# Attention in a two-layer Macaron kernel: the next head's products moved between a head's third scores and its first transposes

## The chip, the cores and the metric

The kernel runs on one core of a Trainium2 chip, in one launch. The metric is the device time of that launch in microseconds (us), the median of several runs. The engines are PE (matrix multiply; PEld is its loading of weights), DVE (vector), ACT (scalar, exponentials and copies), POOL (a second vector engine without access to PE's output banks) and SP (issues transfers). PE writes into PSUM, eight banks of 512 float32 columns each, and DVE and ACT read the results from there.

## The reference

Activations `x` are 1024 tokens of 512 channels, all in float32. Six residual blocks follow each other: a mixture-of-experts FFN, attention, the same FFN again, a LoRA FFN, a Mamba-type scan block, the LoRA FFN again. The change concerns attention alone:

```python
q = einsum('bsd,de->bse', hidden, wq).reshape(B, S, 32, 192)
k, v = ...                       # 32 heads of 128 each, from hidden @ wkv
scores = einsum('bqhd,bkhd->bhqk', q[..., :128], k) * 192 ** -0.5
scores = where(causal, scores, -1e30)
probs = softmax(scores, axis=-1)
attn = einsum('bhqk,bkhd->bqhd', probs, v).reshape(B, S, 32 * 128)
out = einsum('bse,ed->bsd', attn, wo)
```

## The kernel before

The 32 heads go in eight groups of four. The transposed, normalized activations `hT` stay in SBUF. For each group `load_heads` brings four weight tiles (`w_v`, `w_q`, `w_k`, `w_o`) into a pool of four buffers, and POOL forms sums and differences of them (`sums`, L621, and a scaling of `w_q`, L655). `products` (L244 on) computes a 2x2 block product with seven block multiplications in place of eight: each is written to a bank of the small PSUM pool, and DVE (ACT for the first) adds it into the result at L263 to L280.

Per group the values of four heads are computed once (`mm_v`, L795). Per head `products` computes `qT` and `kT` together (`mm_qk`, L819): seven block products of two 128x512 matmuls each. Then come eight query tiles of 128 tokens. For query tile `qt`:

- `scores` (L696) multiplies `qT` with the first `(qt + 1) * 128` keys (L701), in a two-bank tile of the pool `pbig` (two such tiles); DVE adds the causal mask (L708) and takes the negated row maximum (L712); ACT takes the exponential and its row sum (L715); DVE inverts the sum (L716) and scales the probabilities `pr` (L717).
- `attend` (L734) transposes `pr` block by block on PE (L156, up to four blocks in one bank), and copies them to `pT` (L744 on DVE, L746 on ACT). After the fourth and the eighth query tile `values` (L720) multiplies `v` with `pT` (L725) and copies the result to `oT` (L732).

`attend` of a tile runs behind `scores` of the next: the list `pending` holds the tiles not yet attended, and `flush(1)` leaves one of them. After the last tile of a group's fourth head `project_out` (L756) multiplies the four `oT` with `w_o`.

PSUM is split in two pools: `pbig`, two tiles of two banks, for scores alone, and `psml`, four single banks, for all else (products, transposes, outputs, projections). A tile of a pool can only be written when the reader of the tile that had its place is done.

The order on each engine is not the order of the text. A scheduler takes all instructions with their dependences and the order of the text as their priority, assigns the places of the pools, and writes one fixed sequence per engine, in which an instruction may stand ahead of earlier ones that were not ready in its plan. On the chip each engine goes through its sequence in order and waits on semaphores.

## Time and profile before

| | us |
|---|---|
| median of three runs (3053.02 to 3056.49) | 3054.58 |
| the profiled execution | 3056.72 |
| its span, first to last instruction | 3054.9 |
| attention, from the first head's products to the last projection | about 205 to 1721 |
| PE busy in the span | 2861.3 |
| DVE busy in the span | 1719.6 |
| ACT busy in the span | 717.1 |

The profile is one execution, taken on the chip. A row of the groups gives the line, engine and operation, the tiles written and read, the number of instructions, their busy time and mean duration, and the idle time of the engine just before them with what ended it. A row of a timeline gives the start in us from the start of the span, the time until the last instruction of the row ends, and in brackets the idle time before it. A float32 matmul appears as two records. A row of the stages gives the stretch and its length, then busy time and number of instructions of PE, PEld, DVE, ACT and POOL, the granted PE clock as a share of full speed, the share of transfers and their rate.

### The profile page before, as it was taken

The page shows a single profiled execution, that of the slowest core. Times are in us where ns is not written, and L with a number is a line of the kernel's source. Part 1 is how long each engine was busy: PE and PEld are TensorE (multiplying, and loading weights), DVE is VectorE, ACT ScalarE, POOL GpSimd, SP SyncE. Part 2 cuts the span into 40 slices and gives each one's busy share as a digit, 9 for nine tenths or more (in the row PEclk, how much of TensorE's full clock was granted, in tenths as well). Part 3 has the DMA queues.
Part 4 walks back from the last instruction along what each step waited for, and adds up shares of the span by engine and source line. Part 5 has one row for each costly group of instructions (what it writes and reads, how often), then busy time and mean ns, then how long its engine had stood idle before and what let it go on. Part 6 is the DMA issues. An engine that isn't in the chain of part 4 may idle for free.

```text
span 3054.9 us, 29302 instructions
## 1 busy us (share of the span) xinstructions
PE 2861.3 (94%) x10691; PEld 1524.3 (50%) x10691; DVE 1719.6 (56%) x3183; ACT 717.1 (23%) x1381; POOL 790.1 (26%) x601
## 2 busy tenths in 40 slices
PE   5979999999999999999999796899999999999988
PEld 3434645556455554555644343455555555555544
DVE  3156546365463645636445414676776767767673
ACT  1212123031220312203122121422222222222220
POOL 3230101001010010100100123054555545555451
PEclk8989999999999999999999897999999999999999
DMA  8420100001000010000100542222332322323210
GB/s 279 124 72 1 42 14 28 28 1 42 14 28 28 1 42 14 28 28 1 42 14 28 197 131 66 76 90 90 96 97 89 105 90 97 98 88 105 95 42 28
DMA packets 102175, 196.95 MB, mean 64 GB/s; under 512 B 9040, under 2 KB 34800, under 8 KB 102032
## 3 DMA queue, kind: packets, MB, share of 16 engines
q1 hardware_dynamic: 84896, 157.15, 15.8%
q0 software_dynamic: 6240, 20.45, 2.6%
q10 hardware_dynamic: 10896, 17.47, 1.5%
q8 instruction: 87, 1.43, 0.2%
q14 instruction: 56, 0.46, 0.1%
HBM read 176.17 MB, written 18.87 MB: 64 GB/s over the span
## 4 chain that ended last, share of the span: by engine, by line
PE 80%; DVE 10%; POOL 4%; issue 3%; DMA 2%; ACT 1%; POOLq 0%; DVEq 0%; SPq 0%; ACTq 0%
PE ps_in L227 14%; PE ps_m L819 13%; PE ps_o L725 9%; PE ps_wo L760 7%; PE ps_s L701 6%; PE ps_tr L156 6%; PE ps_out L1230 6%; PE ps_m L795 6%; PE ps_e L506 5%; PE ps_y L1186 3%; PE ps_up L238 2%; DVE nm L712 1%; PE ps_st L1204 1%; DVE xc L1039 1%; DVE e_seg L1143 1%
## 5 line engine op out<-in xcount | busy, mean ns | idle before, releaser
L701 PE MATMUL ps_s<-kT,qT 128*128 128x512 f32 (+3 forms) x768 | 305.9, 503 | 33.0 <-ACT pr L715 30.2
L715 ACT ACTIVATE pr<-ps_s,nm 128x128 f32<-128x128 f32 (+7 forms) x256 | 189.7, 741 | 503.7 <-DVE nm L712 444.5
L725 PE MATMUL ps_o<-pT,v 128*128 128x512 f32 (+3 forms) x768 | 266.5, 497 | 1.3 <-ACT pT L746 0.5
L1230 PE MATMUL ps_out<-w_out,yg 128*128 128x512 f32 x512 | 241.6, 616 | 0.0
L227 PE MATMUL ps_in<-hT,w_g 128*128 128x512 f32 x512 | 227.1, 596 | 8.6 <-issue 8.6
L227 PE MATMUL ps_in<-hT,w_x 128*128 128x512 f32 x512 | 225.8, 593 | 0.0
L1168 POOL TENSOR_TENSOR cs<-cT,dd 128x1024 f32<-128x1024 f32 x56 | 181.8, 3247 | 164.9 <-PE ps_y L1186 140.4
L760 PE MATMUL ps_wo<-w_o,oT 128*128 128x512 f32 x512 | 222.1, 592 | 0.0
L725 PEld LDWEIGHTS ps_o<-pT,v 128*128 128x128 f32 x768 | 141.3, 191 | 135.0 <-issue 92.8
L746 ACT COPY pT<-ps_tr 128x256 f32<-128x256 f32 (+2 forms) x192 | 91.9, 479 | 477.8 <-PE ps_tr L156 472.4
L655 POOL TENSOR_SCALAR w_q<-w_q 128x1024 f32<-128x1024 f32 x16 | 44.3, 2770 | 605.8 <-DMA w_q<-in_wq_dram 605.2
L712 DVE TENSOR_REDUCE nm<-ps_s 128x1 f32<-128x128 f32 (+7 forms) x256 | 193.2, 755 | 5.5
L701 PEld LDWEIGHTS ps_s<-kT,qT 128*128 128x128 f32 x768 | 123.3, 190 | 124.7 <-ACT pr L715 65.6
L156 PEld LDWEIGHTS ps_tr<-ident,pr 128*128 128x128 f32 x1152 | 134.3, 141 | 97.5 <-issue 54.1
L156 PE MATMUL ps_tr<-ident,pr 128*128 128x128 f32 x1152 | 164.6, 274 | 19.5 <-DVE pr L717 18.5
L506 PE MATMUL ps_e<-w_all,xt_s 128*128 (+1 forms) x368 | 169.3, 604 | 0.0
L227 PEld LDWEIGHTS ps_in<-hT,w_g 128*128 128x128 f32 x512 | 96.6, 190 | 128.1 <-issue 128.1
L1143 DVE TENSOR_TENSOR_SCAN e_seg<-dd,eye 128x1024 f32<-128x1024 f32 x64 | 154.3, 2411 | 8.6 <-PE ps_y L1186 7.1
L717 DVE TENSOR_SCALAR pr<-pr,sm 128x128 f32<-128x128 f32 (+7 forms) x256 | 155.1, 606 | 4.6
L227 PEld LDWEIGHTS ps_in<-hT,w_x 128*128 128x128 f32 x512 | 97.0, 190 | 120.9 <-issue 120.4
L760 PEld LDWEIGHTS ps_wo<-w_o,oT 128*128 128x128 f32 x512 | 96.2, 190 | 115.7 <-issue 115.7
L1039 DVE SCALAR_TENSOR_TENSOR xc<-ps_in,conv,xc 128x511 f32<-128x511 f32 (+2 forms) x192 | 141.5, 737 | 17.9 <-ACT xc L1035 17.6
(252 smaller groups left out, 4378.1 us busy)
## 6 DMA issues: line engine op xcount, KB each, us to landing
dd<-decay SPq DMA_DIRECT2D x128, 512.0 KB, 4.6
w_all<-in_w_e_dram SPq DMA_DIRECT2D x16, 1024.0 KB, 9.7
outs<-y_e ACTq DMA_DIRECT2D x46, 256.0 KB, 3.5
w_v<-in_wkv_dram SPq DMA_DIRECT2D x8, 1024.0 KB, 5.3
w_q<-in_wq_dram SPq DMA_DIRECT2D x32, 256.0 KB, 4.3
w_k<-in_wkv_dram SPq DMA_DIRECT2D x8, 1024.0 KB, 5.2
w_o<-in_wo_dram SPq DMA_DIRECT2D x8, 1024.0 KB, 5.2
w_x<-in_in_wt_dram SPq DMA_DIRECT2D x8, 1024.0 KB, 7.7
```

The lines of the kernel that those rows point to most:

```text
L156: nc.tensor.transpose(ps[:, i * P : (i + 1) * P], src(i), ident)
L227: nc.tensor.matmul(ps[:, cols : cols + n], lhsT=w[:, k, c0 : c0 + P], rhs=hT[:, k, t0 : t0 + n], start=(k == 0), stop=(k == KT - 1),)
L506: nc.tensor.matmul(ps, lhsT=xt[:, k, :], rhs=w_all[:, bass.ds(ep, 1), k, :].rearrange("p e c -> p (e c)"), start=(k == 0), stop=(k == KT - 1),
L701: nc.tensor.matmul(ps[:, j : j + m], lhsT=qT[:, qt * P : (qt + 1) * P], rhs=kT[:, j : j + m], start=True, stop=True,)
L712: nc.vector.tensor_reduce(nm, ps[:, :n], AX.X, ALU.max, negate=True)
L715: nc.scalar.activation(pr[:, :n], ps[:, :n], AF.Exp, bias=nm, accum_out=sm)
L725: nc.tensor.matmul(ps[:, lo:512], lhsT=v[:, kb, hh * P : (hh + 1) * P], rhs=pT[:, kb, lo:512], start=(kb == 0), stop=(kb == last),)
L760: nc.tensor.matmul(ps, lhsT=heads[hh][:, t * P : (t + 1) * P], rhs=w[:, hh, :], start=(hh == 0), stop=(hh == HG - 1),)
L795: nc.tensor.matmul(ps[:, t * 256 : (t + 1) * 256], lhsT=right[i][:, k, (j + t) * P : (j + t + 1) * P], rhs=left[i][:, k, :], start=(first ...
L819: nc.tensor.matmul(ps, lhsT=left[i][:, k, hh * P : (hh + 1) * P], rhs=right[i][:, k, :], start=(first and k == 0), stop=(last and k == 1), ...
L1143: nc.vector.tensor_tensor_scan(e.rearrange("p h l -> p (h l)"), dd[:, 0, :], eye8.rearrange("p h l -> p (h l)"), 0.0, ALU.mult, ALU.add,)
L1230: nc.tensor.matmul(po, lhsT=yg[:, k, :], rhs=w_o[:, k, :], start=(k == 0), stop=(k == 3))
```

## The change

The loop over groups and heads is turned into one loop over 32 heads, with the work taken apart into `begin_group` (loads, sums, values), `begin_head` (products) and `query_tile`. Three things change in the order and the places:

- The next head's `begin_head` (with the next group's `begin_group` before it where a group ends) is called between the scores of a head's third tile and the first flush behind it.
- Two tiles stay pending in place of one (`flush(2)`).
- Scores of up to 512 columns (the first four tiles) take a single bank of `psml`; only the last four take a two-bank tile of `pbig`.

```diff
             def scores(qT, kT, qt):
                 n = (qt + 1) * P
-                ps = pbig.tile([P, S], F32, tag="pb", name="ps_s")
+                if n > 512:
+                    ps = pbig.tile([P, S], F32, tag="pb", name="ps_s")
+                else:
+                    ps = psml.tile([P, 512], F32, tag="ps", name="ps_s")
...
-            for g in range(AH // HG):
+            def begin_group(g):
+
                 if g == 0:
-                    ld = first
...
+                    return dict(first, v=v_first, heads=[])
+                ld = load_heads(g)
+                v = vp.tile([P, NT, 512], F32, tag="v", name="v")
...
+            def begin_head(gr, g, hh):
+
+                hd = {"gr": gr, "g": g, "hh": hh}
+                hd["qT"] = qT = qkp.tile([P, S], F32, tag="qT", name="qT")
+                hd["kT"] = kT = qkp.tile([P, S], F32, tag="kT", name="kT")
...
+                products(mm_qk, qT[:, :512], qT[:, 512:], kT[:, :512], kT[:, 512:])
...
+            def query_tile(hd, qt, between=None):
+                gr, g, hh = hd["gr"], hd["g"], hd["hh"]
+                if qt % 4 == 0:
+                    hd["pT"] = ptp.tile([P, qt + 4, 512], F32, tag=f"pT{qt}", name="pT")
+                pr = scores(hd["qT"], hd["kT"], qt)
...
+                state["pending"].append((pr, qt, gr["v"], hh, hd["pT"], hd["oT"], done))
+                if between is not None:
+                    between()
+                flush(2)
...
+            def begin(n):
+                g, hh = n // HG, n % HG
+                if hh == 0:
+                    nxt["group"] = begin_group(g)
+                nxt["head"] = begin_head(nxt["group"], g, hh)
+
+            begin(0)
+            for n in range(1, AH + 1):
+                hd = nxt["head"]
+                for qt in range(NT):
+                    query_tile(hd, qt, (lambda: begin(n)) if qt == 2 and n < AH else None)
             flush(0)
```

The engines' sequences for POOL and SP are the same in both programs, line numbers aside. Behind attention those of PE, DVE and ACT are the same too.

More of the change, by code (lines that the diff above doesn't have):

```diff
@@ L671, in attention @@
             state = {"pending": []}
-            v = vp.tile([P, NT, 512], F32, tag="v", name="v")
+            v_first = vp.tile([P, NT, 512], F32, tag="v", name="v")
             def first_v(t):
@@ L676, in first_v @@
                 tokens_times(ps, t, first["wv"], 512)
-                nc.scalar.copy(v[:, t, :], ps)
+                nc.scalar.copy(v_first[:, t, :], ps)
             def pair():
@@ L771, in project_out, with mm_v @@
                     after.flush()
-            for g in range(AH // HG):
+            def begin_group(g):
                 if g == 0:
-                    ld = first
-                else:
-                    ld = load_heads(g)
-                    v = vp.tile([P, NT, 512], F32, tag="v", name="v")
-                    wv = ld["wv"]
-                    left_v = sums(
-                        cp,
-                        wv[:, :2, :256],
-                        wv[:, 2:, :256],
-                        wv[:, :2, 256:],
-                        wv[:, 2:, 256:],
-                        "sv",
-                    )
-                    ld["left"] = left_of_heads(ld, left)
-                wog = ld["wo"]
-                for j in (0, 2) if g else ():
-                    def mm_v(ps, i, first, last, j=j, left=left_v):
+                    return dict(first, v=v_first, heads=[])
+                ld = load_heads(g)
+                v = vp.tile([P, NT, 512], F32, tag="v", name="v")
+                wv = ld["wv"]
+                left_v = sums(
+                    cp,
+                    wv[:, :2, :256],
+                    wv[:, 2:, :256],
+                    wv[:, :2, 256:],
+                    wv[:, 2:, 256:],
+                    "sv",
+                )
+                ld.update(left=left_of_heads(ld, left), v=v, heads=[])
+                for j in (0, 2):
+                    def mm_v(ps, i, first, last, j=j):
                         for t in range(2):
@@ L797, in mm_v @@
                                     lhsT=right[i][:, k, (j + t) * P : (j + t + 1) * P],
-                                    rhs=left[i][:, k, :],
+                                    rhs=left_v[i][:, k, :],
                                     start=(first and t == 0 and k == 0),
@@ L810, in attention @@
                     )
-                left_qk = ld["left"]
-                heads = []
-                for hh in range(HG):
-                    qT = qkp.tile([P, S], F32, tag="qT", name="qT")
-                    kT = qkp.tile([P, S], F32, tag="kT", name="kT")
-                    def mm_qk(ps, i, first, last, hh=hh, left=left_qk):
-                        for k in range(2):
-                            nc.tensor.matmul(
-                                ps,
-                                lhsT=left[i][:, k, hh * P : (hh + 1) * P],
-                                rhs=right[i][:, k, :],
-                                start=(first and k == 0),
-                                stop=(last and k == 1),
-                                skip_group_check=not first,
-                            )
-                    products(mm_qk, qT[:, :512], qT[:, 512:], kT[:, :512], kT[:, 512:])
-                    oT = op.tile([P, S], F32, tag="oT", name="oT")
-                    heads.append(oT)
-                    pT = None
-                    for qt in range(NT):
-                        if qt % 4 == 0:
-                            pT = ptp.tile(
-                                [P, qt + 4, 512], F32, tag=f"pT{qt}", name="pT"
-                            )
-                        pr = scores(qT, kT, qt)
-                        done = None
-                        if hh == HG - 1 and qt == NT - 1:
-                            done = lambda w=wog, hs=heads, last=(g == AH // HG - 1): project_out(w, hs, last)
-                        state["pending"].append((pr, qt, v, hh, pT, oT, done))
-                        flush(1)
@@ new lines, in begin_group, with mm_qk @@
+                return ld
+            def begin_head(gr, g, hh):
+                hd = {"gr": gr, "g": g, "hh": hh}
+                hd["qT"] = qT = qkp.tile([P, S], F32, tag="qT", name="qT")
+                hd["kT"] = kT = qkp.tile([P, S], F32, tag="kT", name="kT")
+                def mm_qk(ps, i, first, last):
+                    for k in range(2):
+                        nc.tensor.matmul(
+                            ps,
+                            lhsT=gr["left"][i][:, k, hh * P : (hh + 1) * P],
+                            rhs=right[i][:, k, :],
+                            start=(first and k == 0),
+                            stop=(last and k == 1),
+                            skip_group_check=not first,
+                        )
+                products(mm_qk, qT[:, :512], qT[:, 512:], kT[:, :512], kT[:, 512:])
+                hd["oT"] = oT = op.tile([P, S], F32, tag="oT", name="oT")
+                gr["heads"].append(oT)
+                return hd
@@ new lines, in query_tile @@
+            def query_tile(hd, qt, between=None):
[3 more added lines that the diff above has]
+                pr = scores(hd["qT"], hd["kT"], qt)
+                done = None
+                if hh == HG - 1 and qt == NT - 1:
+                    done = lambda: project_out(gr["wo"], gr["heads"], g == AH // HG - 1)
+                state["pending"].append((pr, qt, gr["v"], hh, hd["pT"], hd["oT"], done))
+                if between is not None:
+                    between()
+                flush(2)
@@ L843, in attention @@
+            nxt = {}
+            def begin(n):
[8 more added lines that the diff above has]
+                    query_tile(hd, qt, (lambda: begin(n)) if qt == 2 and n < AH else None)
             flush(0)
```

## Prediction

> **What bounds the kernel now.** I read the page first: its engine totals, then the costliest groups with the idle time before each.

> ```profile
> PE 2861.3 (94%) x10691; PEld 1524.3 (50%) x10691; DVE 1719.6 (56%) x3183; ACT 717.1 (23%) x1381; POOL 790.1 (26%) x601
> ...
> L701 PE MATMUL ps_s<-kT,qT 128*128 128x512 f32 (+3 forms) x768 | 305.9, 503 | 33.0 <-ACT pr L715 30.2
> ...
> L156 PE MATMUL ps_tr<-ident,pr 128*128 128x128 f32 x1152 | 164.6, 274 | 19.5 <-DVE pr L717 18.5
> ```

> The kernel is bound by PE. All that attention still gives away is PE's idle time ahead of the scores (33.0 us, they wait for an exponential to free a score buffer) and ahead of the transposes (19.5 us, they wait for the scaled probabilities). The change touches attention alone, so I asked for the stages: 205 us is the first head's products, 1721 us the end of the last output projection.

> ```profile
> 205.00:1721.00 1516.00, 1461.92 (x4942) 803.97 (x4941) 799.28 (x1651) 330.65 (x762) 147.09 (x80) 1.00 0.09 30
> ```

> 1516.0 - 1461.9 = 54.1 us idle is the most that any reordering here can bring. The PE timeline of one head in its steady state (products start at 652.17, the next ones at 686.48: a period of 34.31) shows where a head loses time:

> ```profile
> 664.39 1.04 PE L156 MATMUL ps_tr<-ident,pr 128*128 128x128 f32 x8
> 665.33 0.49 PE L701 MATMUL ps_s<-kT,qT 128*128 128x128 f32 x2
> 665.66 5.86 PE L725 MATMUL ps_o<-pT,v 128*128 128x512 f32 x16
> 671.36 0.60 PE L701 MATMUL ps_s<-kT,qT 128*128 128x256 f32 x2
> 671.79 0.27 PE L156 MATMUL ps_tr<-ident,pr 128*128 128x128 f32 x1
> 671.90 0.81 PE L701 MATMUL ps_s<-kT,qT 128*128 128x384 f32 x2
> 673.62 1.13 PE L701 MATMUL ps_s<-kT,qT 128*128 128x512 f32 x2 [0.91 <-ACT pr L715]
> 674.59 0.38 PE L156 MATMUL ps_tr<-ident,pr 128*128 128x128 f32 x2
> ...
> 676.28 0.52 PE L156 MATMUL ps_tr<-ident,pr 128*128 128x128 f32 x3 [0.24 <-DVE pr L717]
> ```

> I write S0..S7 for a head's eight score tiles, T0..T7 for their transposes. Ends of matmuls are modelled, so I count from start to start: a 128x512 matmul is two records of 0.43, a transpose 0.11. S2 (two records of 0.32) is over at 672.54 and S3 starts at 673.62, its first record 0.11 longer than usual: 1.19 lost. T2 loses 0.40. S5, S6 and the first value matmul lose 0.15, 0.32 and 0.30, and S0 with the last T7 0.17, seen only in start times. Together **2.53 us per head**.

> **Part by part.** Matmuls, transposes, vector and scalar instructions keep their number and shapes; POOL and SP keep their order, and the loads their place. What changes is PE's, DVE's and ACT's order, read off the built programs. In the steady state PE now does: products of the next head, T0, S3, T1, T2, S6, T3, S7 (first half), the first values, T4, S7 (second half), T5, then the next head's S0, T6, S4, S1, first half of S5, T7, second values, S2, products.

> *Removed.* The waits of S3 and T2: the 12.2 us of products now lie between S2 and T0, and cover the exponentials of S0 to S2. Scores up to 512 columns in one bank leave the two double banks to S4..S7, so S4 and S5 are issued before the products.

> *Added: a wait ahead of S6.* It needs a double bank, so S4's exponential. That needs S4's maximum, and DVE has this behind S3's mask and maximum, thus after the products. The chain, durations from this head:

> ```profile
> 664.59 0.69 DVE L280 TENSOR_TENSOR qT<-ps_m,qT 128x512 f32<-128x512 f32 x1 [0.17 <-PE ps_m L819]
> ...
> 675.12 0.69 DVE L712 TENSOR_REDUCE nm<-ps_s 128x1 f32<-128x512 f32 x1
> ...
> 676.42 0.82 DVE L712 TENSOR_REDUCE nm<-ps_s 128x1 f32<-128x640 f32 x1
> ```
> ```profile
> 675.85 0.69 ACT L715 ACTIVATE pr<-ps_s,nm 128x512 f32<-128x512 f32 x1 [0.41 <-DVE nm L712]
> ...
> 677.34 0.79 ACT L715 ACTIVATE pr<-ps_s,nm 128x640 f32<-128x640 f32 x1 [0.71 <-DVE sm L716]
> ```

> Zero is the end of the products (664.39 here). PE: T0 0.11, S3 0.86, T1 and T2 0.55, done at 1.52. DVE: L280 at 0.20; the next instruction 0.61 later (as 671.55 to 672.16) is T0's copy at 0.81. S3 ends at 0.97, its mask starts 0.20 later at 1.17, its maximum 0.33 after that at 1.50, lasting 0.69. S4's maximum starts 0.61 behind it at 2.11 and ends at 2.93. The exponential follows at 2.97 (S3's has released ACT by 2.91), lasts 0.79, and its accumulator read ends 0.09 later, at 3.85. S6 starts 0.05 after such an end and its first record is 0.11 longer: 4.01. The wait is 4.01 - 1.52 = **2.49 us**, one where there were two. T7 is then 0.12 late (S7's mask to scaled probabilities takes 3.97, the issue 0.17 more, against 4.02 of PE work in between), the first values 0.07. Sum 2.68.

> So a steady head goes from 2.53 to 2.68 lost: **+0.15, and 30 heads +4.5 us.** This is the main term; 0.1 us of error in the chain is 3 us in the result. The waits did not go, they were gathered: what is late next is S6, behind DVE's reductions.

> *First head.* Before, nothing hides its softmax: start to start, S0 waits 0.94, S2 0.95, S4 1.35, the first values 0.51, and T7 2.50 (233.63 to 236.13) ahead of the second head's products, 6.25 together. After, the second head's products cover the first three, and the next head's scores T7. It keeps one wait like the one above, at most 2.49; I take 2.3. **-4.0 us.**

> *Last head.* No products follow S2, so T2 and S6 wait as the others' S6 does: 2.5 for 2.53. The wait for the last T7 (3.20 visible) stays. **0.**

> *Behind the waits.* DVE now has S2's mask, maximum and scaling ahead of the products' first add. S2's chain is through 2.4 after S2, the add could start at 1.9: 0.5 late, made up at the next product, 1.72 later. ACT's copy of the first product stands behind S2's exponential and ends with that chain. S0..S3 share the four small banks with products, transposes and outputs; the second product after S2 needs one of them only 1.7 us on, and S1's exponential is long done. Cover 0; if it were gone, up to 0.5 per head.

> *POOL.* Once per group POOL prepares the next weights while DVE scales probabilities, and a scaling that meets a POOL instruction lasts until that one ends:

> ```profile
> 710.03 1.53 DVE L717 TENSOR_SCALAR pr<-pr,sm 128x384 f32<-128x384 f32 x1
> ...
> 713.08 1.02 DVE L717 TENSOR_SCALAR pr<-pr,sm 128x512 f32<-128x512 f32 x1
> ```

> Undisturbed they take 0.41 and 0.47. Before, this adds 0.24 to a T1 and 0.7 to a T2, 0.94 per group. After, POOL's sums start 5.5 us behind the products and last 10: they meet the scalings of S5 and S6 (7 and 8.5 behind), which have 2 us before T5 and T6 need them. I take 0.8 per group, bounds 0 and 2: over seven groups **-1 us, between -6.6 and +7.4**.

> Sum: +4.5 - 4.0 - 1 = -0.5, **no change**. The profiled execution took 3056.72 (span 3054.9), 2.1 above the median of 3054.58; on the median the forecast is 3054.1.

> [...] The clock first. The granted clock is 1.00 around the 2.34 us wait at 236 us, but falls after the 3.20 us wait of the last head (between the last S7 and the values PE has only 15 transposes for 5.4 us):

> ```profile
> 233.60:239.00 5.40, 3.06 (x13) 1.78 (x13) 3.66 (x7) 2.26 (x6) 0.00 (x0) 1.00 0.00 0
> ...
> 1678.40:1682.00 3.60, 3.58 (x5) 1.70 (x6) 0.51 (x1) 0.00 (x0) 0.11 (x1) 0.55 0.00 0
> ```

> By the rows, 3.29 us without a real matmul (233.63 to 236.92, transposes included) kept the clock, 5.4 lost it. The new stretch, S3's end to S6, is 0.55 + 2.49 = 3.04, so I charge nothing. [...]

> **Rivals.**
> *The clock drops behind S6's wait (slower).* Price by the trace: four value matmul records from 1678.42 took 3.39 where they take 1.72, 1.67 us. If a quarter of the 31 heads pay, +13: 3067; if all, +52: 3106. It decides once stretches without matmuls exceed somewhere between 3.3 and 5.4 us. Chance 0.06.
> *DVE becomes the bound behind S6 (slower).* If POOL meets four scalings and not two, 1.1 us each, 4.4 less 2 of slack is 2.4 per group, +1.5 net, seven times +10: 3065. Likewise if the chain of S6 is 0.35 longer than worked out. Chance 0.16.
> *The gathered wait is shorter (faster).* If S4's exponential ended 0.4 earlier: -12, 3042. For it: every link is a fixed latency that may overlap more. Against: DVE's order is fixed, and all links are measured in sequence. Chance 0.13.
> *The change does what its words promise in full:* all 54 us gone, 3000. The order of DVE, with S4's maximum behind the products, speaks against it: 0.01.
> *No change,* as summed: 0.64.

> **The numbers.** A measurement of this kernel can tell 0.2%, 6.1 us. Faster 0.14, within it 0.64, slower 0.22. Likeliest 3054.1. The range takes in 0.2 us of error in the head's chain (6 us) with POOL's bounds, and toward the slow side the DVE rival: 3046 to 3066.

> **What would show it.** In the profile after: the idle time ahead of S3 and T2 gone; one idle stretch per head ahead of the 128x512 scores, 2.2 to 2.4 visible, released by ACT's exponential; a steady period of 34.4 to 34.5; the second head's products about 14.6 us after the first's; PE's clock 1.00 in attention; idle time in attention still 50 to 56 us. Wrong if the wait of S6 is under 2.0 or over 2.8, or if clock rows below 1.00 appear in each head.

## The result, and the profile after

The changed kernel takes **3069.49 us** (median; 3066.68 to 3072.3) against 3054.58 before: the ratio is 1.0048, with a 95% interval of 1.0033 to 1.0063. It is slower by more than the 0.2% that a measurement can tell, and 3.5 us above the upper end of the forecast's range. The profiled execution took 3069.49 us, its span is 3067.8.

The page after: the engine totals, then the two groups that the prediction started from.

```profile
PE 2853.0 (93%) x10691; PEld 1527.8 (50%) x10691; DVE 1708.5 (56%) x3183; ACT 715.6 (23%) x1381; POOL 793.7 (26%) x601
...
L704 PE MATMUL ps_s<-kT,qT 128*128 128x512 f32 (+3 forms) x768 | 303.9, 503 | 66.6 <-ACT pr L718 66.6
...
L156 PE MATMUL ps_tr<-ident,pr 128*128 128x128 f32 x1152 | 168.3, 277 | 12.7 <-DVE pr L720 4.7
```

The waits were gathered as worked out: 66.6 us ahead of the scores where there were 33.0, and 12.7 ahead of the transposes where there were 19.5. 66.6 is 30 waits of 2.22, one in each head but the first and the last. The stage of attention (the length; then busy us of PE, PEld, DVE, ACT, POOL; then the PE clock), with its end set 12 us later than before, as the last projection ends at 1733.7 and not at 1720.9:

```profile
205.00:1733.00 1528.00, 1448.29 (x4937) 805.95 (x4936) 788.88 (x1650) 328.35 (x761) 148.24 (x80) 0.99 0.09 30
```

The clock has gone from 1.00 to 0.99. The PE timeline shows the same wait in two heads, the first as in most heads, the second as in a few:

```profile
655.39 1.77 PE L704 MATMUL ps_s<-kT,qT 128*128 128x512 f32 x4 [2.22 <-ACT pr L718]
656.99 0.60 PE L156 MATMUL ps_tr<-ident,pr 128*128 128x128 f32 x4
657.43 1.02 PE L704 MATMUL ps_s<-kT,qT 128*128 128x512 f32 x2
...
689.88 2.08 PE L704 MATMUL ps_s<-kT,qT 128*128 128x512 f32 x4 [2.22 <-ACT pr L718]
691.75 1.06 PE L156 MATMUL ps_tr<-ident,pr 128*128 128x128 f32 x4
692.61 1.92 PE L704 MATMUL ps_s<-kT,qT 128*128 128x512 f32 x2
```

The wait is equal to the hundredth. Behind the second one four transposes take 0.86 us to the next start in place of 0.44, and two records of a 128x512 score 1.71 in place of 0.86. Stretches behind the two places (the clock is the third number from the end):

```profile
691.21:694.61 3.40, 3.40 (x9) 1.94 (x8) 2.80 (x6) 1.86 (x5) 2.71 (x2) 0.50 0.00 1
655.30:658.80 3.50, 3.41 (x11) 1.75 (x12) 3.13 (x8) 1.75 (x5) 0.00 (x0) 1.00 0.00 0
```

PE runs at half speed for a stretch of 3.41 us that begins 1.1 to 1.4 us behind the end of the wait. This happens behind five of the 30 waits (at 271, 691, 814, 1200 and 1620 us) and in the last head behind a wait of 2.11 us (at 1678); before the change only the very last wait (3.20 us) had it, and still has. A steady head without it has a period of 34.49 us, a head with it 36.09. Four of the five are steady heads. The one at 691 stands at a change of group: its period of 61.11 is hardly longer than the others' there (60.74 to 61.04), probably since the half clock takes the place of a wait for DVE that PE's rows have at the six other changes of group and not at this one.

### The profile page after: what moved, and what is told of

Its sections match the earlier page's. It is cut to its first block, busy times and chain, and to the rows that moved or that the text cites. A ratio compares the mean times of both kernels' runs of the same rounds, so it can differ in the third digit from the quotient of the medians.

```text
span 3067.8 us, 29291 instructions
## 1 busy us (share of the span) xinstructions
PE 2853.0 (93%) x10691; PEld 1527.8 (50%) x10691; DVE 1708.5 (56%) x3183; ACT 715.6 (23%) x1381; POOL 793.7 (26%) x601
## 4 chain that ended last, share of the span: by engine, by line
PE 80%; DVE 9%; POOL 4%; issue 3%; ACT 2%; DMA 2%; POOLq 0%; ACTq 0%; DVEq 0%; SPq 0%
PE ps_in L227 14%; PE ps_m L823 13%; PE ps_o L728 8%; PE ps_s L704 7%; PE ps_wo L763 7%; PE ps_out L1251 6%; PE ps_m L797 6%; PE ps_tr L156 5%; PE ps_e L506 5%; PE ps_y L1207 3%; ACT pr L718 2%; PE ps_up L238 2%; DVE nm L715 1%; PE ps_st L1225 1%; DVE pr L720 1%
## 5 line engine op out<-in xcount | busy, mean ns | idle before, releaser
L704 PE MATMUL ps_s<-kT,qT 128*128 128x512 f32 (+3 forms) x768 | 303.9, 503 | 66.6 <-ACT pr L718 66.6
L715 DVE TENSOR_REDUCE nm<-ps_s 128x1 f32<-128x128 f32 (+7 forms) x256 | 189.7, 751 | 3.3
L156 PEld LDWEIGHTS ps_tr<-ident,pr 128*128 128x128 f32 x1152 | 135.9, 143 | 94.1 <-issue 52.1
L156 PE MATMUL ps_tr<-ident,pr 128*128 128x128 f32 x1152 | 168.3, 277 | 12.7 <-DVE pr L720 4.7
L632 POOL TENSOR_TENSOR sv<-w_v 128x512 f32<-128x512 f32 x7 | 8.9, 1266 | 622.3 <-DMA w_v<-in_wkv_dram 622.3
```

Of the source, the lines that this page charges most:

```text
L156: nc.tensor.transpose(ps[:, i * P : (i + 1) * P], src(i), ident)
L704: nc.tensor.matmul(ps[:, j : j + m], lhsT=qT[:, qt * P : (qt + 1) * P], rhs=kT[:, j : j + m], start=True, stop=True,)
L715: nc.vector.tensor_reduce(nm, ps[:, :n], AX.X, ALU.max, negate=True)
```

## The experiments

The theory: most of the extra time is the clock, which drops behind S6's wait in some heads; the rest is the wait's 0.15 to 0.2 us per head and POOL's lengthened scalings, less the first head's gain. The rivals: POOL and DVE are late and the half-clock stretches are a side effect; or the time lies in the gathered wait itself. "Replay" in the expectations means each engine's built order, run forward on paper with durations from the trace and a constant clock.

**Four extra matmuls inside the wait.** They stand behind T2's transposes and write the unused quarter of that bank:

```diff
                     ps = transposes(...)
+                    if qt == 2:
+                        for _ in range(4):
+                            nc.tensor.matmul(ps[:, 3 * P :], lhsT=ident, rhs=pr[:, :P], start=True, stop=True)
```

> The changed kernel, with four extra 128x128 float32 matmuls behind the third tile's transposes of each head (into the unused quarter of the same bank, read by nobody). They lie inside PE's wait ahead of the seventh score tile (2.22 us visible) and take about 0.22 us each, 0.86 together, so that the wait's idle part falls to about 1.4 us and S6 itself starts as before. Clock theory (after's extra time is mostly six stretches of 1.6 to 1.7 us at half clock behind this wait, 9.9 us together): no stretch below full clock in attention but the last head's, every head 34.5 us, 3069.5 - 9.9 = about 3059.5. Rival, DVE and POOL lateness, or the wait as such: PE does more work and waits no less, 3069 to 3070, and the stretches at half clock are either still there or were not what costs.

3061.48 us, ratio to before 1.0021 (1.0011 to 1.0030). More work, no wait's cause taken away, and about 8 us faster than the change. The page, and the same head as the second one above:

```profile
L704 PE MATMUL ps_s<-kT,qT 128*128 128x512 f32 (+3 forms) x768 | 298.0, 495 | 40.0 <-ACT pr L718 39.8
```
```profile
686.12 1.06 PE L746 MATMUL ps_tr<-pr,ident 128*128 128x128 f32 x8
688.50 1.77 PE L704 MATMUL ps_s<-kT,qT 128*128 128x512 f32 x4 [1.33 <-ACT pr L718]
690.11 0.60 PE L156 MATMUL ps_tr<-ident,pr 128*128 128x128 f32 x4
```

The fill takes up part of the wait (66.6 us became 40.0), S6 starts where it did, and the four transposes behind it take 0.44 again. In attention only the last head still shows half clock. Every steady period is 34.49, as in the heads of the change that keep the full clock, so this kernel is the change with the clock's cost alone taken away: attention (first product to last projection) lasts 1521.95 us, against 1528.92 with the change and 1515.25 before (to the start of the last projection).

**Two extra matmuls** (the same with `range(2)`):

> The same with two extra matmuls, 0.43 us, idle part about 1.8 us and, with the transposes ahead of it, a good 2.0 us of a 3.41 us window without matmuls that count. Clock theory: in after only the waits that fell whole into one window (S6 starts at 0.35 to 0.64 us of it) were followed by half clock; shortened by 0.43 us there should be none or one or two left in place of six: 3059 to 3063. Rival (lateness, or the wait as such): 3069 to 3070.

3061.2 us, 1.0025 (1.0015 to 1.0035), no half clock but in the last head (the granted clock of attention is 1.00): none of the waits, here 1.77 us, was followed by it.

**Eight extra transposes** in the same place, in place of matmuls (`nc.tensor.transpose(ps[:, 3 * P :], pr[:, :P], ident)`):

> The changed kernel with eight extra transposes (0.11 us each, 0.87 together, read by nobody) at the place where the four extra matmuls stood. If transposes count for the clock as matmuls do (in the three kernels with half-clock stretches before this run, a single bound of some 1.3 us of PE work per 3.41 us window, transposes counted in full, parts the windows before such a stretch from all others), there is no such stretch in a steady head and the time is that of the four extra matmuls, 3059 to 3064. If transposes do not count, the stretches are as frequent as in the changed kernel, 5 to 8 in attention, 3067 to 3072.

3059.41 us, 1.0018 (1.0009 to 1.0027), no half clock in a steady head: 0.87 us of transposes did the same here as 0.86 us of matmuls. No run bears out counting transposes with the idle time, as the expectation of two extra matmuls does to come to 2.0 us.

**POOL taken out** of the change and of before. For groups 2 to 8 the sums and the scaling of `w_q` are left out and raw tiles used:

```diff
+        if later is None:
+            return {1: a11, 2: a12, 3: a12, 4: a22, 5: a21, 6: a11, 7: a21}
...
-        for half in (wqg[:, :2, :], wqg[:, 2:, :]):
+        for half in () if later is None else (wqg[:, :2, :], wqg[:, 2:, :]):
```

> The changed kernel without POOL's work for groups 2 to 8: the sums and differences of the weights and the scaling of w_q are left out (raw tiles go in their place, so this part of the computation is changed). If POOL costs the 0.9 us of idle ahead of T6 and T7 that the rows show per group, plus what the lengthened scalings shift, replaying the built order with measured durations gives some 11 us less than after: 3058 to 3060. The clock theory expects the stretches at half clock to remain in a like share of the heads (4 to 7 of 31, 1.6 to 1.7 us each). If POOL is the cause of the 15 us (rival), this kernel is at least 10 us closer to its counterpart made from the kernel before than after is to before.

> The kernel before, with the same part left out. Replay with measured durations: 12 us less than before, 3042 to 3044, thus as much as in the changed kernel, and the difference between the two stays 10 to 16 us by the clock theory. By the rival (POOL meets the scalings in a worse place after the change) before loses little here, 0 to 4 us, and the two kernels without POOL come within 5 us.

3065.56 (1.0036, 1.0022 to 1.0050) and 3046.2 (0.9971, 0.9960 to 0.9982): 19 us apart, more than with POOL. POOL as the cause of the 15 us falls; a share is left to it. The first number missed its expectation because ten heads fell to half clock and not four to seven, the second by 2 us. The periods of a group (one first projection to the next) give the share of POOL, with 1.6 us taken off for a half-clock stretch: without POOL 189.26 before and 189.99 after (191.59 - 1.6), with POOL 190.57 before and 191.83 in the change with the fill (means of six groups). POOL thus costs 1.31 per group before and 1.84 after the change: +0.53. DVE's timeline in the kernel with four extra matmuls shows how:

```profile
691.65 1.36 DVE L720 TENSOR_SCALAR pr<-pr,sm 128x768 f32<-128x768 f32 x1
692.94 0.15 DVE L719 RECIPROCAL sm<-sm 128x1 f32<-128x1 f32 x1
693.20 2.52 DVE L720 TENSOR_SCALAR pr<-pr,sm 128x896 f32<-128x896 f32 x1
695.64 0.68 DVE L735 COPY oT<-ps_o 128x512 f32<-128x512 f32 x1
```
```profile
696.38 0.44 PE L156 MATMUL ps_tr<-ident,pr 128*128 128x128 f32 x2 [0.72 <-DVE oT L735]
```

The scalings of S5 and S6 meet POOL's sums, as worked out (1.36 and 2.52 us, against 0.61 and 0.69 in the changed kernel without POOL; two of POOL's sums run here from 690.22 to 692.60 and from 692.68 to 695.24), and T5 and T6 had time for that. But the copy of the first values stands behind them on DVE, and its bank is the one that T5's second half needs (T5 has six transposes, four and then these two). This wait comes in all seven groups, 5.1 us together, 0.73 of the 1.84 per group; the rest of POOL's share isn't traced to single waits.

**The parts, one by one.** The second pending tile alone, and the single banks alone, each put into the kernel before:

```diff
-                        flush(1)
+                        flush(2)
```
```diff
-                ps = pbig.tile([P, S], F32, tag="pb", name="ps_s")
+                if n > 512:
+                    ps = pbig.tile([P, S], F32, tag="pb", name="ps_s")
+                else:
+                    ps = psml.tile([P, 512], F32, tag="ps", name="ps_s")
```

> The kernel before with one line changed: flush(2) in place of flush(1), nothing else. If the second pending tile is the useful part of the change and the place of the products the harmful one, this is faster than both: a replay of the built order with durations of the trace gives 17 us less than before, 3036 to 3042, waits of at most 0.9 us in a steady head and therefore no stretch at half clock in attention but the last head's. If the three parts only help together (rival), it is no faster than before: 3050 to 3070.

> The kernel before with only the scores of up to 512 columns moved to single banks of the small pool. Replay: 67 us more than before, 3115 to 3130 at full clock, since these scores then compete with transposes and outputs for four banks and one wait ahead of a 128x512 score grows to 3.1 us in each head. Clock theory: a wait of 3.1 us is beyond the 2.2 us that already drops the clock at some places of the window, so most heads show a stretch at half clock, 1.6 to 1.7 us each: a further 25 to 50, 3140 to 3170. Rival (what counts for the clock is a gap of a whole window, or something other than the gap): 3115 to 3130.

3050.56 (0.9989, 0.9979 to 0.9998) and 3186.78 (1.0430, 1.0413 to 1.0448). The pending tile gains a little, but misses what the replay had: the steady period is 33.92, but the heads at a group's change take 60.8 for 60.1. The banks alone are far worse, above the expectation's upper end.

Then the change without one part, all scores in two-bank tiles again, or one pending tile:

> The changed kernel with all scores in two-bank tiles again; the products stay between the third scores and the first transposes and two tiles stay pending. Replay: 21 us more than after at full clock, with waits of 0.8, 1.7 and 1.0 us per head, none as long as 2.2. Clock theory: no stretch at half clock in a steady head, so the 21 us are set off by some 8 to 10 us saved: 3078 to 3084. Without the clock theory: 3090.

> The changed kernel with flush(1) in place of flush(2). Replay: 77 us more than after's warm time, one wait of 3.1 us and one of 1.1 us per head: 3137 at full clock (3060 + 77). Clock theory: most heads are followed by a half-clock stretch after the 3.1 us wait, 20 to 31 of 1.6 to 1.7 us: 3165 to 3190. Rival: 3137 to 3147.

3093.72 (1.0134, 1.0114 to 1.0155) and 3168.83 (1.0376, 1.0359 to 1.0394). The second is as expected. Of 31 waits of 2.90 us 24 are followed by half clock, six of these for twice the usual length and at about twice the loss, 3.0 us. The records behind one run at half speed:

```profile
685.93 2.07 PE L704 MATMUL ps_s<-kT,qT 128*128 128x512 f32 x2 [2.90 <-ACT pr L718]
687.80 1.06 PE L156 MATMUL ps_tr<-ident,pr 128*128 128x128 f32 x4
```

The first missed: I expected no half clock, since no wait is as long as 2.2, and eight heads ahead of the last have it. Without these, eight times 1.6, it would be near 3081 and within the range. Its PE timeline corrects the theory:

```profile
275.60 0.39 PE L701 MATMUL ps_s<-kT,qT 128*128 128x128 f32 x2
277.50 0.96 PE L156 MATMUL ps_tr<-ident,pr 128*128 128x128 f32 x7 [1.51 <-DVE pr L717]
278.29 0.60 PE L701 MATMUL ps_s<-kT,qT 128*128 128x256 f32 x2
279.66 1.65 PE L701 MATMUL ps_s<-kT,qT 128*128 128x384 f32 x2 [0.77 <-ACT pr L715]
```

Half clock begins at 279.24. The 3.41 us ahead of that hold the wait of 1.51 and the first 0.35 of the wait of 0.77, with 1.4 us of work between them (277.50 to 278.89). No single gap reached 2.2: the clock fell here behind two shorter ones close together.

Last, before with **two of the parts** (`flush(2)` and the single banks, the products where they were):

> The kernel before with two of the three parts, flush(2) and the single banks for short scores, the products left where they were. If the place of the products is the harmful part, this is faster than before: replay 23 us less, one wait of 1.0 us per head; as the replay was 13 us too low for the second pending tile alone, 3032 to 3046. If the single banks are harmful whatever else is done (alone they cost 132 us), 3070 or more.

3045.28, 0.9971 (0.9961 to 0.9981). So the single banks are no harm beside a second pending tile, and of the three parts it is the place of the products that made the change slower than before: it alone parts this kernel from the change, 24 us apart.

**The products one and two tiles later.**

```diff
-                    query_tile(hd, qt, (lambda: begin(n)) if qt == 2 and n < AH else None)
+                    query_tile(hd, qt, (lambda: begin(n)) if qt == 4 and n < AH else None)
```

> The changed kernel with one number changed: the next head's products are called behind the scores of a head's fifth tile in place of the third. S3's and S4's maxima then stand ahead of the products' adds on DVE, so that S4's exponential lies under 12 us of matmuls and S6 finds its double bank free. Theory (S6's wait behind DVE's reductions, and the clock that falls in it, are the whole cost; pending and banks are no harm): replay of the built order gives no wait above 0.25 us in a steady head but one of 1.3 us per group, 73 us less than before, 2985 to 2995, no stretch at half clock in a steady head. Rival (POOL, or DVE's total load, is what counts): DVE has the same work and POOL the same collisions, so the waits come back elsewhere, 3040 to 3070.

> The same with the products behind the fourth tile: S3's maximum ahead of them, S4's still behind. Replay: S6's wait falls from 2.2 to 0.73 us, and one wait of 2.3 us per group stays; 47 us less than before, 3008 to 3018, no stretch at half clock in a steady head and at most two or three behind the one wait per group. Rival: 3040 to 3070.

Behind the fourth tile 3007.02 (0.9850, 0.9835 to 0.9865), 1 us under its range; behind the fifth **2988.53** (0.9786, 0.9772 to 0.9799), 2.1% less than before and 2.6% less than the change. Of the latter, its page, its stage of attention, and DVE at the start of a head's products (650.25 on PE):

```profile
PE 2831.1 (95%) x10691; PEld 1524.3 (51%) x10691; DVE 1717.7 (57%) x3183; ACT 707.3 (24%) x1381; POOL 796.5 (27%) x601
...
L704 PE MATMUL ps_s<-kT,qT 128*128 128x512 f32 (+3 forms) x768 | 287.6, 490 | 0.0
...
L156 PE MATMUL ps_tr<-ident,pr 128*128 128x128 f32 x1152 | 165.0, 275 | 20.6 <-DVE sm L719 11.4
```
```profile
205.00:1660.00 1455.00, 1433.33 (x4971) 805.86 (x4970) 800.66 (x1658) 321.77 (x765) 153.83 (x92) 1.00 0.10 32
```
```profile
650.57 0.69 DVE L715 TENSOR_REDUCE nm<-ps_s 128x1 f32<-128x512 f32 x1
651.17 0.15 DVE L719 RECIPROCAL sm<-sm 128x1 f32<-128x1 f32 x1
651.24 0.80 DVE L715 TENSOR_REDUCE nm<-ps_s 128x1 f32<-128x640 f32 x1
...
652.37 0.94 DVE L715 TENSOR_REDUCE nm<-ps_s 128x1 f32<-128x768 f32 x1
```

The maxima of S3, S4 and S5 (128x512, 128x640, 128x768) stand ahead of the products' first add, under 12 us of matmuls. S6's bank is free long before S6, the scores wait for nothing, and the steady period is 31.92. What idles is at the group changes, where the last tiles still wait for DVE, and in the last head.

## Why the prediction was wrong

In attention of the profiled executions the change costs 1528.92 - 1515.25 = 13.7 us (the whole spans are 12.9 apart, the medians 14.9). By the prediction's own terms:

| term | predicted | measured | from |
|---|---|---|---|
| 30 steady heads | +4.5 | +5.6 | 34.49 less 34.31 = 0.185, 30 times |
| first head | -4.0 | -4.2 | what the other rows leave of 13.7 |
| last head | 0 | +1.6 | one half-clock stretch that before lacked, at the price of a steady head |
| POOL | -1 | +3.7 | +0.53 per group, seven times |
| clock behind S6 | 0 | +7.0 | change less change with fill |

The first head is the one term without a measurement of its own. Its rows after the change show no wait ahead of S6, but one of 1.19 us ahead of T3 and one of 0.34 ahead of T6, where the prediction left 2.3.

**The step that failed is the clock charged at nothing.** It cost 7.0 us behind S6 and some 1.6 in the last head; with the clock held by the fill the time was 3061.48, inside the forecast's range. The step measured stretches without a real matmul and took 3.04 us as safe because 3.29 us had kept the clock at 236 us. Both halves of that were wrong. With 0.87 us of extra transposes in the wait the clock stayed at 1.00 in every steady head, so in these kernels the quantity to look at was the idle time, 2.2 to 2.5 us in both places. And one place that keeps its clock proves nothing. The prediction's own sentence "wrong if clock rows below 1.00 appear in each head" set the wrong test too: they appear in one head of six, which is the rival with "a quarter of the 31 heads" at 1.67 us each, given a chance of 0.06 and 3067 us. Its price was right, as a head with half clock takes 1.60 more; the point from which it was to decide, over 3.3 us without matmuls, was not.

What parts the heads is position. Take S6's start modulo 3.413 us, the length of the half-clock stretches: in the change the five waits that were followed by half clock lie at 0.35 to 0.64, the 25 others at 0 to 0.17 and 1.97 to 3.24. In the changed kernel without POOL the ten are at 1.50 to 2.12, and all 20 others outside. The position is in the trace: it holds the time of every change of the clock, and in each of the 14 executions profiled here all of them lie whole multiples of 3.413 us apart, to 0.003 us (25 changes in the kernel before, 37 in the change). So I cut PE's records at these places into slices of that length. The slices ahead of half clock and ahead of full clock, for the two waits of the change shown above, and the slice around the wait at 236 us before the change:

```profile
687.79:691.20 3.41, 1.32 (x4) 0.71 (x5) 3.37 (x8) 2.43 (x7) 2.68 (x1) 1.00 0.80 285
653.66:657.06 3.40, 1.67 (x5) 0.88 (x6) 3.16 (x8) 2.61 (x6) 0.00 (x0) 1.00 0.00 0
```
```profile
234.41:237.82 3.41, 1.69 (x10) 1.24 (x11) 2.56 (x5) 1.68 (x3) 0.00 (x0) 1.00 0.00 0
```

The first slice holds 2.09 us of its wait. The other two hold 1.73 of 2.22 and 1.72 of 2.34, the rest fell into the slice before. That may be why the place at 236 us kept its clock; no run set the position itself.

I counted PE's work in every such slice of attention but the last head's, in all 14 executions, from start to start (0.43 us for a 512-column record, less in proportion) and with transposes in full. All 78 full-clock slices with less than 1.25 us of work were followed by half clock, and none of some 5800 with more than 1.38 was; between the two 3 of 26 were. In the change alone the five slices ahead of half clock hold 0.97 to 1.25 us, and the next, with 1.28, kept the clock; in the kernel before the lowest holds 1.30 and none lost it. (The busy time in the rows is larger, as it holds the modelled ends of matmuls.) With transposes left out the count doesn't part them: in the change a slice with 0.73 us then kept the clock, and one with 0.97 lost it.

In the change one wait of 2.22 us in six was followed by half clock; two gaps of 1.51 and 0.77 us together were too (all scores in two-bank tiles), and waits of 1.77 us were not (two extra matmuls).

**POOL was mis-sized,** -1 for +3.7, within its bounds of -6.6 to +7.4. Before the change, too, POOL took 1.31 per group and not the 0.94 that was read from the waits. That it meets the scalings of S5 and S6 was right. What was left out, as far as it is traced, is DVE's queue behind them: the copy of the first values, and the bank that waits for it.

**Right:** the chain of S6. 4.01 - 1.52 = 2.49 from start to start has a visible part of 2.22 in the rows, in all 30 heads that have it; the steady period came out at 34.49, within 34.4 to 34.5; the waits of S3 and T2 are gone from a steady head; the second head's products start 14.6 us after the first's. One sign missed: idle time in attention is 1528.00 - 1448.29 = 79.7 us and not 50 to 56. Before, only 1.15 of a head's loss of 2.53 showed as idle (0.91 and 0.24); after, 2.22 does, and 30 of that are 66.6. The sentence "the waits did not go, they were gathered" describes the kernel. That the gathered wait is worse than its sum is what the clock added.

## What to carry to other kernels

## What the runs showed of the hardware that I had not expected

- Adding 0.4 to 0.9 us of useless matmuls or transposes per head made the changed kernel 8 to 10 us faster (3061.48, 3061.2 and 3059.41 against 3069.49): the half-clock stretches of its steady heads, 1.60 us of a period each, were gone.
- In all 14 executions the changes of the clock lie whole multiples of 3.413 us apart, and a wait of 2.22 us was followed by half clock where 2.09 us of it lay in one slice of that length, and not where 1.73 did. With POOL's delays gone ten of 30 heads were hit and not five, at the same wait; the delays shift the heads against these slices, but that this is the reason was not tested.
- A half-clock stretch of 3.413 us costs a steady head 1.5 to 1.7 us whether the wait ahead of it was 2.2 or 2.9 us. Six of the 31 waits of 2.90 us are followed by twice that length, and seven by none.
